# Cross-attention block on one core: the shift of b1 by four transfers ahead of the first feed-forward, first-layer chunks moved around transposes, and a last step with context and low scores together

## The chip, the core and the metric

The kernel runs on one core of a Trainium2 chip. A core has five instruction streams: TensorE (PE, with PEld for its weight loads), VectorE (DVE), ScalarE (ACT), GpSimd (POOL) and SyncE (SP, which here only issues transfers). SP and ACT each issue DMAs on a queue of their own. The metric is device microseconds of one execution; lower is better.

## The reference, cut to what matters

128 independent sequences of 128 tokens with 256 features, 16 heads of 16, a feed-forward of 1024, all in float32. The mask lets a query attend only to strictly earlier keys, and token 0 attends to nothing.

```python
q = (query @ Wq + bq); k = (key @ Wk + bk); v = (values @ Wv + bv)      # split in 16 heads
scores = jnp.einsum('bhqd,bhkd->bhqk', q, k) / jnp.sqrt(jnp.float32(D_K))
allowed = j < i + mask                                                  # mask == 0
attn = jax.nn.softmax(jnp.where(allowed, scores, NEG_INF), axis=-1)
attn = attn.at[:, :, 0, :].set(0.0)
ctx = jnp.einsum('bhqk,bhkd->bhqd', attn, v)
x = layer_norm(query + ctx @ Wo + bo, ln1_g, ln1_b)
ffn = jax.nn.relu(x @ W1 + b1) @ W2 + b2
out = layer_norm(x + ffn, ln2_g, ln2_b)
```

## The kernel before

Two sequences form a pair p; there are 64 pairs (NP = 64). The order of instructions on every engine is written out by hand: the calls in the source are the order of each engine's stream, and nothing reorders them. Each stream is worked off in order, so an instruction that waits holds back all that stands behind it on its engine, DMA issues included.

Work is pipelined over pairs. `step(p)` (line 785, p = 2 to 62) computes the scores and the softmax of pair p, the context, output projection and first norm of pair p-1, the first feed-forward layer of pair p-2 and the second layer and last norm of pair p-3; it also projects queries, keys and values of pair p+1. Lines 671 to 776 are the start-up (pairs 0 and 1), lines 885 to 971 the last step (pair 63) and what drains the pipeline behind it. The pieces named below are:

- `scores(p, hi)`, L326: `hi` = 1 is the upper half of the queries (128 keys), `hi` = 0 the lower half (64 keys). Then `mask` (DVE, L345), `maximum` (DVE L356, POOL L357), `exponential` (ACT, L364), `sums` (DVE L376 and L377, POOL L378).
- The probabilities are transposed. In the loop DVE does it in blocks of 32 (`turn`, L391, tile `tb`) and `bring` (L406) moves the blocks into `pT` by 16 DMAs, eight issued by SP and eight by ACT. For pairs 0, 1 and 63 `turn_on_pe` transposes on PE (L421) and ACT copies the result into `pT` (L423).
- `weigh` (L438, L448) multiplies `pT` with the values into `pc`; its first matmuls already read the lower half's part of `pT`. `context` (L460) copies `pc` to `cxT` on ACT, `attention_out` (L467) projects it, `attention_sum` and `attention_stats` (DVE, POOL) and `norm1` (DVE, L507) follow.
- `turn_x1` transposes the normed tile on DVE and by DMAs (x1t L237, x1T L240); `turn_x1_on_pe` (L226 on PE, copies on ACT L623 for pair 0, L628 else) is used for pairs 0 and 63.
- `hidden(p, fs)` (L638) is the first layer, two 128-wide chunks of the 1024 to one PSUM bank (eight matmuls as the trace counts them), with bias and relu on ACT (L644). `second` (L656) is the second layer; `second_sum`, `stats`, `scale_and_shift` (POOL: ve, sd, nb; L487, L488, L528), `norm2` (ACT, L536), `finish` (POOL, L542 and L543) and `store` (a DMA issued by ACT, L551) end a pair.

The first norm's gain and shift are folded into the first layer: W1 is scaled in place by `scale_w1` in step 3, and b1 gets be1 @ W1 added. `fold_norm1` computes be1 @ W1 by matmuls with one output row each (L566, 16 as the trace counts them), four side by side, and copies the four rows to `b1s` on ACT (L572). `add_b1` brings the 1024 numbers into a column layout `b1e_c` [128, 8] by eight DMAs on SP (L578). Pair 0 uses the unscaled W1 and the plain b1; the first reader of `b1e_c` is an addition on POOL in step 3 (L831). In step 2 both calls stand behind `scores(2, 0)`, and the first layer of pair 0 is cut in two: chunks 0 to 3 between the start-up's transposes, chunks 4 to 7 at the end of the step.

PSUM tiles of one bank come from a pool of four in turn (`bank`), those of two banks from a pool of two (`pair`). The built program gives every SP and ACT transfer one of eight completion semaphores in turn, in the order in which transfers stand in one list for both queues. A transfer waits at its issue until the one eight places before it in this list has landed, on whichever queue that was.

Of the kernel before, what the change touches and what calls it, by code (L numbers as in the profile page):

```python
# [10 lines left out]
ALU = mybir.AluOpType  # L11
AX = mybir.AxisListType

P = 128
NEG_INF = -1e30
LN_EPS = 1e-5
# [3 lines left out]
def tile_cross_attention_block(  # L20
# [22 lines left out]
    nc = tc.nc  # L43
# [308 lines left out]
    def maximum(p, hi, part):  # L352
        st = states[p]
        n = P if hi else HP
        sm, nmx = st["sm", hi], st["nmx", hi]
        nc.vector.tensor_reduce(nmx[:, part], sm[:, part, :], AX.X, ALU.max, negate=True)  # L356
        nc.gpsimd.tensor_tensor(  # L357
            sm[:, part, :], sm[:, part, :],
            nmx[:, part, None].to_broadcast([P, part.stop - part.start, n]), ALU.add,
        )  # L360

    def exponential(p, hi, part):
        sm = states[p]["sm", hi]
        nc.scalar.activation(sm[:, part, :], sm[:, part, :], AF.Exp)  # L364
# [132 lines left out]
    def attention_stats(p):  # L497
        stats(p, states[p]["t1"], 1)
        deviation(p, 1)
# [59 lines left out]
    def fold_norm1():  # L559


        ps = bank("ps_b1")
        n = DFF // NS
        for k in range(KC):
            for j in range(NS):
                nc.tensor.matmul(  # L566
                    ps[32 * j : 32 * j + 1, :n], be1_c[:, k : k + 1],
                    w1[:, k, j * n : (j + 1) * n], start=(k == 0), stop=(k == KC - 1),
                )
        for j in range(NS):  # L570
            at = slice(32 * j, 32 * j + 1)
            nc.scalar.copy(b1s[at], ps[at, :n])  # L572

    def add_b1():

        for f in range(FC):
            j, u = f // 2, f % 2
            nc.sync.dma_start(  # L578
                b1e_c[:, f : f + 1], b1s[32 * j : 32 * j + 1, u * P : (u + 1) * P]
            )  # L580

    def scale_w1():
# [30 lines left out]
    def turn_x1_on_pe(p):  # L613
        st = states[p]
        x1T = ffn.tile([P, NS, 4 * 32], F32, tag="x1T", name=f"x1T_{p}")
        st["x1T"] = x1T.rearrange("p i (s k a) -> p s i k a", s=2, k=KC)
        pt = transposed(st["x1"], f"ptn_{p}").rearrange(
            "p (k s i a) -> p k s i a", k=KC, s=2, i=NS
        )
        for k in range(KC):  # L620
            if p == 0:

                nc.scalar.activation(  # L623
                    st["x1T"][:, :, :, k, :], pt[:, k], AF.Identity,
                    bias=be1_c[:, k : k + 1], scale=g1_c[:, k : k + 1],
                )
            else:
                nc.scalar.copy(st["x1T"][:, :, :, k, :], pt[:, k])  # L628

    def hidden(p, fs, between=None):  # L630
        st = states[p]
        if fs[0] == 0:
            st["hT"] = ffn.tile([P, FC, TP], F32, tag="hT", name=f"hT_{p}")
        for f in fs[::2]:
            ph = bank(f"ph_{p}_{f}")
            for i in range(2):
                for k in range(KC):
                    nc.tensor.matmul(  # L638
                        ph[:, i * TP : (i + 1) * TP].rearrange("p (s i a) -> p s i a", s=2, a=32),
                        w1[:, k, (f + i) * P : (f + i + 1) * P], st["x1T"][:, :, :, k, :],  # L640
                        start=(k == 0), stop=(k == KC - 1),
                    )
            for i in range(2):
                nc.scalar.activation(  # L644
                    st["hT"][:, f + i, :], ph[:, i * TP : (i + 1) * TP], AF.Relu,
                    bias=(b1e_c if p else b1_c)[:, f + i : f + i + 1], scale=1.0,
                )
            if between:
                between(f)
# [135 lines left out]
    def step(p):  # L785
        nonlocal waiting
        if p > 2:
            load_ahead(p)
        scores(p, 1)
        mask(p, 1, 0)  # L790
        maximum(p, 1, ONE)
        if p > 2:
            second(p - 3, 0)
            mask(p, 1, 1)
            maximum(p, 1, TWO)
            exponential(p, 1, ONE)
            second(p - 3, 1)
            if p + 2 < NP:
                tokens(p + 2, "c")
        else:  # L800
            turn_x1_on_pe(0)
            hidden(0, range(FC // 2))
            turn_on_pe(1, 1, range(2))
            mask(p, 1, 1)
            maximum(p, 1, TWO)
            exponential(p, 1, ONE)
            turn_on_pe(1, 1, range(2, 4))
            turn_on_pe(1, 0, range(2))
            for which in "xc":
                tokens(3, which)  # L810
            add_bo(1)
            load_ahead(2)
            load_tokens(2)
        summed = []
        sums(p, 1, ONE)
        exponential(p, 1, TWO)
        if p > 2:
            second_sum(p - 3)
            summed = [p - 3]
        sums(p, 1, TWO)  # L820


        weigh(p - 1)
        context(p - 1)
        scores(p, 0)
        if p == 2:
            fold_norm1()
            add_b1()
        if p == 3:
            scale_w1()  # L830
            nc.gpsimd.tensor_tensor(b1e_c, b1e_c, b1_c, ALU.add)  # L831
        queries(p + 1)
        mask(p, 0, 0)
        mask(p, 0, 1)
        maximum(p, 0, ALL)
        exponential(p, 0, ALL)
        turn(p, 1, 0)
        turn(p, 1, 1)
        for q in waiting:
            finish(q)  # L840
        if p == 2:
            add_bo(2)
        attention_out(p - 1)
        attention_sum(p - 1)
        sums(p, 0, ALL)
        attention_stats(p - 1)
        if p + 2 < NP:
            tokens(p + 2, "x")
            if p == 2:
                tokens(p + 2, "c")  # L850
        turn(p, 0, 0)
        bring(p, nc.sync, range(NS * NS // 2))
        keys(p + 1)
        norm1(p - 1)
        turn_x1(p - 1)
        values(p + 1)
        values_out(p + 1)
        for q in waiting:
            store(q)
        add_bo(p + 1)  # L860
        if p == 2:
            residual1(0)
        residual1(p - 1)
        for q in summed:
            stats(q, states[q]["t2"], 2)
        for q in summed:
            scale_and_shift(q)
        at = NS * NS // 2

        def share(f):  # L870
            nonlocal at
            n = NS * NS - at if f == FC - 2 else 0 if f == 0 or p == 2 else NS // 2
            bring(p, nc.scalar, range(at, at + n))
            at += n

        hidden(p - 2, range(0 if p > 2 else FC // 2, FC), share)
        for q in summed:
            norm2(q)
        waiting = summed
# [5 lines left out]
    p = NP - 1  # L885
# [3 lines left out]
    second(p - 3, 0)  # L889
    mask(p, 1, 1)  # L890
    maximum(p, 1, TWO)
    scores(p, 0)
    mask(p, 0, 0)
    mask(p, 0, 1)
    exponential(p, 1, ONE)
    maximum(p, 0, ALL)
    exponential(p, 1, TWO)
    second(p - 3, 1)
    sums(p, 1, ONE)
    sums(p, 1, TWO)  # L900
    second_sum(p - 3)
    exponential(p, 0, ALL)
    sums(p, 0, ALL)
    finish(p - 4)
    weigh(p - 1)
    context(p - 1)
    attention_out(p - 1)
    attention_sum(p - 1)
    attention_stats(p - 1)
    norm1(p - 1)  # L910
    turn_x1(p - 1)
# [1 line left out]
    residual1(p - 1)  # L913
    stats(p - 3, states[p - 3]["t2"], 2)
    scale_and_shift(p - 3)
    hidden(p - 2, range(FC))
    turn_on_pe(p, 1, range(4))
    norm2(p - 3)

# [10 lines left out]
    attention_sum(p)  # L930
    attention_stats(p)
    second_sum(p - 2)
    hidden(p - 1, range(FC))
    norm1(p)
    stats(p - 2, states[p - 2]["t2"], 2)
    turn_x1_on_pe(p)
    residual1(p)
    scale_and_shift(p - 2)
    hidden(p, range(FC // 2))
# [15 lines left out]
    for s in range(2):  # L955
        py = bank(f"py_last_{s}")
        for f in range(FC):
            nc.tensor.matmul(
                py[:, :D], st["hT"][:, f, s * P : (s + 1) * P], w2[:, f, :],
                start=(f == 0), stop=(f == FC - 1),  # L960
            )
        nc.vector.tensor_tensor(t2[:, s], py[:, :D], st["x1b"][:, s], ALU.add)
        bs = small.tile([P, 6], F32, tag="bs", name=f"bs_last_{s}", bufs=4)
        mv = small.tile([P, 2], F32, tag="mvl", name=f"mv_last_{s}")
        nc.vector.bn_stats(bs, t2[:, s])
        nc.vector.bn_aggr(mv, bs)
        sd = small.tile([P, 1], F32, tag="sdl", name=f"sd_last_{s}")
        nc.gpsimd.tensor_scalar(sd, mv[:, 1:2], LN_EPS, None, ALU.add)
        nc.gpsimd.tensor_tensor(sd, sd, power[:, 0], ALU.pow)
        norm_alone(t2[:, s], mv[:, 0:1], sd)  # L970
        nc.sync.dma_start(out[2 * NP - 2 + s], t2[:, s])
# [35 lines left out]
```

## Time and profile before

| what | value |
|---|---|
| median of three runs | 1601.18 us (1600.74 to 1602.05) |
| profiled execution | 1598.13 us |
| its span, first to last instruction | 1596.4 us |
| PE busy | 1574.0 us, 99% of the span |
| DVE busy | 1372.2 us, 86% |
| POOL busy | 1282.6 us, 80% |
| ACT busy | 755.9 us, 47% |
| mean granted TensorE clock | 0.998 |
| distance of two steps in the loop (first-layer starts at 1471.58 and 1495.85) | 24.27 us |
| from the first matmul of `pc` to the first layer, in the loop (1510.84 to 1519.95) | 9.11 us |
| the same in step 3 (76.55 to 87.20) | 10.65 us |

A row of the timeline has the start and the duration in microseconds, the engine, the source line, the operation, output and inputs with their sizes, how many instructions are merged in it, and in brackets the idle time before it with what ended it. PE, PEld, DVE, ACT and POOL are the engines' work; SPq and ACTq are the issuing of DMAs. A wait is put down to the releaser that came last by the profile.

### The profile page before, as it was taken

The page shows a single profiled execution, that of the slowest core. Times are in us where ns is not written, and L with a number is a line of the kernel's source. Part 1 is how long each engine was busy: PE and PEld are TensorE (multiplying, and loading weights), DVE is VectorE, ACT ScalarE, POOL GpSimd, SP SyncE. Part 2 cuts the span into 40 slices and gives each one's busy share as a digit, 9 for nine tenths or more (in the row PEclk, how much of TensorE's full clock was granted, in tenths as well). Part 3 has the DMA queues.
Part 4 walks back from the last instruction along what each step waited for, and adds up shares of the span by engine and source line. Part 5 has one row for each costly group of instructions (what it writes and reads, how often), then busy time and mean ns, then how long its engine had stood idle before and what let it go on. Part 6 is the DMA issues. An engine that isn't in the chain of part 4 may idle for free.

```text
span 1596.4 us, 41271 instructions
## 1 busy us (share of the span) xinstructions
PE 1574.0 (99%) x16512; PEld 1327.7 (83%) x16512; DVE 1372.2 (86%) x1988; ACT 755.9 (47%) x1498; POOL 1282.6 (80%) x1106
## 2 busy tenths in 40 slices
PE   8899999999999999999999999999999999999998
PEld 6688888888888888888888888888888888888887
DVE  7889898888888998898988988888888889889862
ACT  5554454454444444444545444544444455454442
POOL 6878888888887888888888888878878888888882
PEclk9999999999999999999999999999999999999999
DMA  9356656556556556565565565565555655654430
GB/s 195 84 134 136 150 128 137 138 117 155 133 130 146 126 137 156 130 137 135 128 146 146 120 143 141 120 156 131 132 140 123 146 146 133 144 132 109 115 85 26
DMA packets 480511, 210.12 MB, mean 132 GB/s; under 512 B 349248, under 2 KB 448832, under 8 KB 480320
## 3 DMA queue, kind: packets, MB, share of 16 engines
q1 hardware_dynamic: 371952, 134.55, 37.9%
q10 hardware_dynamic: 108368, 72.92, 17.6%
q8 instruction: 131, 2.15, 0.6%
q14 instruction: 60, 0.49, 0.1%
HBM read 70.00 MB, written 33.03 MB: 65 GB/s over the span
## 4 chain that ended last, share of the span: by engine, by line
PE 95%; POOL 1%; DVE 1%; ACT 1%; DMA 1%; issue 0%; SPq 0%; POOLq 0%; ACTq 0%; DVEq 0%
PE ph L638 27%; PE py L656 27%; PE pq L260 8%; PE po L467 7%; PE pk L260 7%; PE pv L292 7%; PE pss L326 6%; PE pc L448 4%; PE pc L438 2%; POOL sm L357 0%; POOL sm L378 0%; ACT pT L423 0%; DMA pT<-tb 0%; DVE nmx L356 0%; DVE sm L345 0%
## 5 line engine op out<-in xcount | busy, mean ns | idle before, releaser
L357 POOL TENSOR_TENSOR sm<-sm,nmx 128x1024 f32<-128x1024 f32 x192 | 364.2, 1897 | 122.0 <-DVE nmx L356 121.1
L638 PE MATMUL ph<-x1T,w 128*128 128x256 f32 x2048 | 453.0, 379 | 2.4 <-ACT x1T L623 1.6
L656 PE MATMUL py<-w,hT 128*128 128x256 f32 x2016 | 452.8, 382 | 0.0
L378 POOL TENSOR_TENSOR sm<-sm,rs 128x1024 f32<-128x1024 f32 x192 | 364.3, 1899 | 93.6 <-DVE rs L377 89.6
L656 PEld LDWEIGHTS py<-w,hT 128*128 128x128 f32 x2016 | 377.6, 190 | 72.8 <-issue 16.7
L638 PEld LDWEIGHTS ph<-x1T,w 128*128 128x128 f32 x2048 | 388.9, 190 | 55.8 <-ACT x1T L623 2.0
L644 ACT ACTIVATE hT<-ph,b1e_c 128x256 f32<-128x256 f32 x504 | 208.2, 471 | 206.1 <-PE ph L638 104.8
L364 ACT ACTIVATE sm<-sm 128x1024 f32<-128x1024 f32 x192 | 200.8, 1054 | 206.5 <-POOL sm L357 206.1
L376 DVE TENSOR_REDUCE su<-sm 128x8 f32<-128x1024 f32 (+1 forms) x192 | 233.7, 1217 | 69.7 <-ACT sm L364 67.5
L345 DVE TENSOR_TENSOR sm<-pss,neg 128x1024 f32<-128x1024 f32 (+1 forms) x256 | 235.2, 940 | 52.2 <-PE pss L326 51.9
L391 DVE STREAM_TRANSPOSE tb<-sm 128x1024 f32<-128x1024 f32 x183 | 220.0, 1227 | 28.1 <-POOL sm L378 28.1
L356 DVE TENSOR_REDUCE nmx<-sm 128x8 f32<-128x1024 f32 (+1 forms) x192 | 234.3, 1220 | 6.6
L536 ACT ACTIVATE t<-t,nb,sd 128x256 f32<-128x256 f32 x124 | 67.7, 593 | 187.4 <-DMA pT<-tb 124.7
L260 PE MATMUL pq<-xT,wq 128*128 128x256 f32 x512 | 127.6, 392 | 0.0
L467 PE MATMUL po<-wo,cxT 128*128 128x256 f32 x512 | 121.2, 379 | 1.5 <-ACT cxT L460 1.4
L282 ACT ACTIVATE kT<-pk,bkh,half 128x256 f32<-128x256 f32 x252 | 120.6, 558 | 1.4 <-PE pk L260 1.4
L292 PE MATMUL pv<-wv,cT 128*128 128x256 f32 x512 | 121.0, 379 | 0.0
L260 PE MATMUL pk<-cT,wk 128*128 128x256 f32 x504 | 119.2, 379 | 0.0
L326 PE MATMUL pss<-kT,qT 32*64 32x256 f32 (+1 forms) x4096 | 116.8, 335 | 0.4 <-ACT kT L705 0.2
L271 ACT ACTIVATE qT<-pq,bqs_c 128x256 f32<-128x256 f32 x128 | 53.6, 470 | 122.8 <-PE pq L260 122.8
L260 PEld LDWEIGHTS pq<-xT,wq 128*128 128x128 f32 x512 | 92.4, 190 | 21.0 <-issue 10.9
L515 POOL TENSOR_TENSOR x1b<-x,g_r 128x512 f32<-128x512 f32 x64 | 81.7, 1277 | 34.9 <-DVE x L507 34.9
(92 smaller groups left out, 1765.9 us busy)
## 6 DMA issues: line engine op xcount, KB each, us to landing
pT<-tb ACTq DMA_DIRECT2D x488, 96.0 KB, 2.7
pT<-tb SPq DMA_DIRECT2D x488, 96.0 KB, 2.9
out_dram<-t ACTq DMA_DIRECT2D x63, 256.0 KB, 2.5
xb<-in_x_dram SPq DMA_DIRECT2D x124, 128.0 KB, 4.4
cb<-in_ctx_dram SPq DMA_DIRECT2D x124, 128.0 KB, 4.4
x<-in_x_dram SPq DMA_DIRECT2D x31, 512.0 KB, 4.9
x1t<-tbx SPq DMA_DIRECT2D x248, 64.0 KB, 2.3
x1T<-x1t SPq DMA_DIRECT2D x62, 256.0 KB, 3.2
```

What stands on the lines that cost most here:

```text
L260: nc.tensor.matmul(ps[:, m * TP : (m + 1) * TP], w[:, k, m * P : (m + 1) * P], src[:, k, :], start=(k == 0), stop=(k == KC - 1),)
L292: nc.tensor.matmul(pv[:, s * D : (s + 1) * D], st["cT"][:, k, s * P : (s + 1) * P], wv[:, k, :], start=(k == 0), stop=(k == KC - 1),)
L326: nc.tensor.matmul(sps[r // 2][s * HP : (s + 1) * HP, r % 2, m * 2 * n : (m + 1) * 2 * n].rearrange("p (e j) -> p e j", e=2), st["qT"][str ...
L345: nc.vector.tensor_tensor(st["sm", hi][:, part, :].rearrange("p (r n) j -> p r n j", r=2), st["sps", hi][t][:, :, : 4 * n].rearrange("p r ...
L356: nc.vector.tensor_reduce(nmx[:, part], sm[:, part, :], AX.X, ALU.max, negate=True)
L357: nc.gpsimd.tensor_tensor(sm[:, part, :], sm[:, part, :], nmx[:, part, None].to_broadcast([P, part.stop - part.start, n]), ALU.add,)
L376: nc.vector.tensor_reduce(su, sm[:, part, :], AX.X, ALU.add)
L378: nc.gpsimd.tensor_tensor(sm[:, part, :], sm[:, part, :], rs[:, :, None].to_broadcast([P, part.stop - part.start, n]), ALU.mult,)
L391: nc.vector.transpose(st["tb"][:, :, at : at + 256].rearrange("p j (n a) -> p n j a", a=32), st["sm", hi].rearrange("p h j -> p (h j)")[:, ...
L467: nc.tensor.matmul(po[:, s * D : (s + 1) * D], cxT[:, k, s, :], wo[:, k, :], start=(k == 0), stop=(k == KC - 1),)
L638: nc.tensor.matmul(ph[:, i * TP : (i + 1) * TP].rearrange("p (s i a) -> p s i a", s=2, a=32), w1[:, k, (f + i) * P : (f + i + 1) * P], st[ ...
L656: nc.tensor.matmul(st["py"][:, s * D : (s + 1) * D], st["hT"][:, f, s * P : (s + 1) * P], w2[:, f, :], start=(f == 0), stop=(f == FC - 1),)
```

## The change

Six edits, the first three in the start-up's step 2, the others at the end:

1. `fold_norm1` reads the moving operand in another order: columns u*128 + p of a quarter of W1 as (p, u), so that two consecutive elements lie 128 floats apart. The row in PSUM then has the two numbers of one partition side by side.
2. `add_b1` issues four DMAs in place of eight, each with two floats to a partition.
3. In step 2 both calls stand ahead of the first layer of pair 0 and behind the first two of pair 1's six transposes on PE; chunks 4 and 5 of that first layer move from the end of the step to a place before pair 1's last two transposes. On SP the four DMAs of b1 now stand ahead of the loads of the next inputs.
4. In the last step `second(60, 1)`, `weigh(62)` and `context(62)` stand ahead of `scores(63, 0)`, as in the loop; the first layer of pair 61 is cut, four chunks before `attention_out(62)` and four behind it; on POOL the lower half's subtraction and division stand later, the division behind `finish(59)`.
5. Behind it the transpose of pair 63's normed tile (`turn_x1_on_pe`) stands ahead of the last two chunks of pair 62's first layer.
6. In the last two norms the addition of epsilon goes from POOL to DVE.

```diff
@@ fold_norm1, add_b1
-                    ps[32 * j : 32 * j + 1, :n], be1_c[:, k : k + 1],
-                    w1[:, k, j * n : (j + 1) * n], start=(k == 0), stop=(k == KC - 1),
+                    ps[32 * j : 32 * j + 1, :n].rearrange("o (p u) -> o p u", p=P),
+                    be1_c[:, k : k + 1],
+                    w1[:, k, j * n : (j + 1) * n].rearrange("d (u p) -> d p u", p=P),
+                    start=(k == 0), stop=(k == KC - 1),
...
-        for f in range(FC):
-            j, u = f // 2, f % 2
+        for j in range(NS):
             nc.sync.dma_start(
-                b1e_c[:, f : f + 1], b1s[32 * j : 32 * j + 1, u * P : (u + 1) * P]
+                b1e_c[:, 2 * j : 2 * j + 2],
+                b1s[32 * j : 32 * j + 1].rearrange("o (p u) -> o p u", p=P),
             )
@@ step
             turn_x1_on_pe(0)
+            turn_on_pe(1, 1, range(2))
+            fold_norm1()
+            add_b1()
             hidden(0, range(FC // 2))
-            turn_on_pe(1, 1, range(2))
             mask(p, 1, 1)
             maximum(p, 1, TWO)
             exponential(p, 1, ONE)
             turn_on_pe(1, 1, range(2, 4))
+            hidden(0, range(FC // 2, 3 * FC // 4))
             turn_on_pe(1, 0, range(2))
...
-        if p == 2:
-            fold_norm1()
-            add_b1()
...
-        hidden(p - 2, range(0 if p > 2 else FC // 2, FC), share)
+        hidden(p - 2, range(0 if p > 2 else 3 * FC // 4, FC), share)
@@ the last step
     maximum(p, 1, TWO)
+    exponential(p, 1, ONE)
+    second(p - 3, 1)
+    sums(p, 1, ONE)
+    exponential(p, 1, TWO)
+    second_sum(p - 3)
+    sums(p, 1, TWO)
+    weigh(p - 1)
+    context(p - 1)
     scores(p, 0)
     mask(p, 0, 0)
     mask(p, 0, 1)
-    exponential(p, 1, ONE)
     maximum(p, 0, ALL)
-    exponential(p, 1, TWO)
-    second(p - 3, 1)
-    sums(p, 1, ONE)
-    sums(p, 1, TWO)
-    second_sum(p - 3)
+    hidden(p - 2, range(FC // 2))
     exponential(p, 0, ALL)
-    sums(p, 0, ALL)
     finish(p - 4)
-    weigh(p - 1)
-    context(p - 1)
     attention_out(p - 1)
     attention_sum(p - 1)
+    sums(p, 0, ALL)
     attention_stats(p - 1)
...
-    hidden(p - 2, range(FC))
+    hidden(p - 2, range(FC // 2, FC))
...
-    hidden(p - 1, range(FC))
+    hidden(p - 1, range(FC - 2))
     norm1(p)
     stats(p - 2, states[p - 2]["t2"], 2)
     turn_x1_on_pe(p)
+    hidden(p - 1, range(FC - 2, FC))
...
-        nc.gpsimd.tensor_scalar(sd, mv[:, 1:2], LN_EPS, None, ALU.add)
+        nc.vector.tensor_scalar(sd, mv[:, 1:2], LN_EPS, None, ALU.add)
```

In the last step p is 63. Behind the piece shown, both versions go on with `turn_on_pe(63, 1, range(4))`, `norm2(60)`, `turn_on_pe(63, 0, range(2))`, `finish(60)`, `store(60)`, `second(61, 0)`, `weigh(63)`. The order inside the loop for p = 3 to 62 is the same in both.

## The prediction

> **What bounds the kernel now.** I read the page's busy rows and chain first, then PE's waits, then the timeline where those waits fall, and last the granted clock there.
>
> ```profile
> PE 95%; POOL 1%; DVE 1%; ACT 1%; DMA 1%; issue 0%; SPq 0%; POOLq 0%; ACTq 0%; DVEq 0%
> ```
>
> The chain that ended last is PE. The loop repeats every 24.27 us with PE full, and no edit changes its order; only PE's waits in the start-up and the last steps can be won. All of PE's waits from the change's places:
>
> ```profile
> PE pc L438 <- DMA x1t<-tbx: 3.9, 1, 3.9
> ...
> PE pc L438 <- ACT pT L423: 2.3, 4, 1.7
> PE ph L638 <- ACT x1T L623: 1.6, 1, 1.6
> ...
> PE po L467 <- ACT cxT L460: 1.4, 1, 1.4
> PE ph L638 <- ACT x1T L628: 0.8, 1, 0.8
> ```
>
> Columns: total, times, longest. The largest, 3.9 us, is in step 3; its named releaser is a guess, since `pc` reads pT, not x1t. The timeline says what it is:
>
> ```profile
> 54.40 15.23 SPq L578 DMA_DIRECT2D b1e_c<-b1s  x8
> ...
> 69.73 5.12 SPq L406 DMA_DIRECT2D pT<-tb  x8
> ...
> 76.55 0.43 PE L438 MATMUL pc<-pT,vd 128*32 128x64 f32 x16 [3.89 <-DMA x1t<-tbx]
> ```
>
> The eight transfers of b1 hold SP until 69.63, though tb was complete at 63.87 (last transpose 62.67 + 1.20). SP's eight pT transfers follow; the last is issued at 69.73 + 5.12 - 0.6 = 74.25, and `pc` starts 2.3 us later. Most of the 15 us is one wait, for `vd` of pair 3:
>
> ```profile
> SPq L578 <- DMA vd<-vz: 8.9, 1, 8.9
> ```
>
> That is the rule of eight semaphores in turn. After the wait the clock is low (columns: window, length, PE busy, granted clock, DMA share, GB/s):
>
> ```profile
> 76.00:77.00 1.00, 0.45 (x33) 1.00 0.57 135
> 77.00:78.00 1.00, 1.00 (x57) 0.56 0.56 140
> 78.00:79.00 1.00, 1.00 (x41) 0.50 0.01 1
> 79.00:80.00 1.00, 1.00 (x33) 0.50 0.03 3
> 80.00:81.00 1.00, 1.00 (x4) 0.73 0.00 0
> ```
>
> From `pc` to the first layer step 3 takes 10.65 us, the loop 9.11: 1.54 us more.
>
> **Edits 1 to 3, before `pc` of step 3.** Before, PE waits 1.64 us at 42.29 for x1T. Now the 8 transposes (0.93 us) and the fold (0.97 us from 52.90 to the next start) stand there. The fold's bank is free at 41.77 (copies of pv), so it runs 41.85 to 42.8, beside x1T (until 42.69). Chunks 0 to 5 and the other transposes fill PE until 49.9. But ACT now does four b1s copies (1.53 us) and chunks 4 and 5 (0.84 us) ahead of pT's last copies: x1T to 42.69, two pT copies 43.8, b1s 45.3, hT 47.4, exponential 48.5, two copies 49.5, hT 50.3, two copies 51.35 against 50.76. So `pc(1)` ends 0.6 us later, but the fold (0.97) behind it is gone: queries(3) start at 53.45 against 53.87, and with chunks 4, 5 gone (1.73 us) scores(3) start at 62.3 against 64.43 and the second layer ends at 70.45 against 72.63. PE is 2.15 us ahead; its work was never the limit there.
>
> What is late next is the transfer of pT(2). exponential(2, 1, TWO) follows pT's copies on ACT, so sums, low mask and tb on DVE end at 64.5 (63.87 + 0.65). SP is then free: the b1 transfers are issued from 44 to 46.5, after each b1s copy; the loads behind them wait for DVE's transposes at 47.96 anyway, and the x load (one wait more, for the first xb load) goes out by 53. Cover gone, these cost nothing until 64.
>
> By the built program's order the list of transfers now reads vd(3), A1, a load, A2, A3, the x load, A4, A5, S1, A6, S2, A7, S3, A8, S4 to S8 (A and S: pT transfers of ACT and SP). Each waits for the eighth before it: S1 for vd(3), S3 for A3, S4 for A4, S5 for A5, S7 for A6. The old trace gives 2.4 us from issue to release (A1 at 64.60, A4, which waited for it, at 66.99) and 0.65 us per issue. A1 goes at 64.55, A3 at 66.0; S1 at 64.75 (vd 62.0 + 2.7), S2 65.4, S3 not before 66.0 + 2.4 = 68.4, then one per 0.65: S8 at 71.6. `pc(2)` starts at 71.6 + 2.27 = 73.9 instead of 76.55: **-2.65 us**, where a free SP queue would have given 5. PE idles 70.45 to 73.9, 3.45 us.
>
> Two prices are not in the trace. **The strided read of W1:** the nearest row is the fold with contiguous reads,
>
> ```profile
> 52.90 1.04 PE L566 MATMUL ps_b<-w,be_c 128*1 128x256 f32 x16
> ```
>
> that is 0.97 us. The Trainium skill, "SBUF — State Buffer", section "Door 1: The DMA port swizzle (why `[64,N]` ≈ `[32,N]`)", speaks against the edit: two successive accesses must fall into the same 16-byte line for full bandwidth, and here none do. By the row the sum is 0, by the rule, estimated as twice the time, +0.97, all of it on the path since ACT's b1s copies and the first layer follow. A gain is excluded, as no matmul is removed. I take 0, the only measured row; range 0 to +1.
>
> **The clock:** low from 76.9 to 80.3 after 3.89 us of idling, not low after 1.64 and 1.68. The Trainium skill, "TensorE: Matmul & The Clock Gate", section "Part 1: The HAM clock gate (the "warmup" mystery)", states half clock after an idle window of about 3.4 us, with windows running free. By the rule taken strictly 3.45 us would almost never hold a whole window, and 1.54 more would go; by the trace the window before the drop (3.4 us up to 76.9) held 0.4 us of work, so a not quite idle window is enough and 3.45 can trip it as 3.89 did. I take the row: 0, with -1.54 as the other end.
>
> **Edit 4, last step.** It begins as before at 1526.95, and up to the low scores it now stands as the loop's: `pc(62)` 1535.1, low scores 1536.6, chunks 0 to 3 of pair 61 at 1537.2 (its x1T, issued 1533.07, has 3.3 us of landing), po at 1540.67 without the 1.43 us wait for cxT, transposes at 1545.95 instead of 1547.79: 1.84 us early. They and the first half of the second layer end at 1552.2. (From here on the leading 15 is left out.) Then `pc(63)` needs ACT's last two pT copies, and these stand behind `norm2(60)`:
>
> ```profile
> 1551.28 0.50 POOL L528 TENSOR_SCALAR nb<-mv,sd 128x1 f32<-128x1 f32 x2
> ...
> 1551.58 1.09 ACT L536 ACTIVATE t<-t,nb,sd 128x256 f32<-128x256 f32 x2 [0.57 <-POOL nb L528]
> 1552.58 1.04 ACT L423 COPY pT<-ptp 128x512 f32<-128x512 f32 x2
> ...
> 1554.22 0.43 PE L438 MATMUL pc<-pT,vd 128*32 128x64 f32 x16
> ```
>
> nb ends POOL's row, and POOL starts it later: the low half's chain is now max 38.76 to 39.98, subtraction to 41.96, exponential to 43.04, then DVE's t1 sum (po ends 42.56) to 43.25, sum and reciprocal to 44.7, while POOL does `finish(59)` to 44.56; division 44.86 to 46.76, ve, sd to 47.83, DVE's norm 48.6, x1b to 51.35, ve(60) at 51.31 against 50.15: 1.16 us late. (All durations are the same lines' rows of before.) `norm2(60)` at 52.74, copies done 54.78 against 53.62. The rest of `pc(63)` follows, and the next matmul starts at 54.83 + 1.47 (the same stretch at 50.81 to 52.28) = 56.30 against 55.70. The stall of 1.43 goes, one of 2.1 comes: **+0.6 us**. If POOL were early enough the step would give -1.84; if 2.1 us of idling lowered the clock, +2.1.
>
> **Edits 5 and 6.** From the first layer of pair 62 to that of pair 63 it is 8.27 us (1560.98 to 1569.25); now 32 matmuls (6.91) and four transposes (0.5), the copies of x1T (0.65) lying beside the last chunk: 7.4, **-0.87**. Epsilon on POOL takes from 1591.88 to the power at 1592.48, with a hop of 0.28 before; on DVE the nearest row is a 128x2 tensor_scalar at 0.16 us: about -0.4 for each of two norms. The second norm's add (1590.70) follows directly on the first's last operation while PE has ended at 1590.23, so both count: **-0.8**, between -0.3 (DVE waits for PE) and -0.9.
>
> **Sum:** -2.65 + 0.6 - 0.87 - 0.8 = -3.7 us against the profiled 1598.13 (span 1596.4 and 1.73 around it): 1594.4. The median shown is 3.05 above the profiled run; the same difference on it gives **1597.5 us**.
>
> **Rivals.** *The clock holds:* 3.45 us of idling stays under the gate, or SP is a little quicker: -3.7 - 1.54 = -5.2, 1596.0. For it the strict rule, against it the window above. *The last step pays:* POOL's chain is 1.2 us shorter than I count, `pc(63)` waits for nothing: 2.4 more, 1595.1; against it the idle of 0.57 that ACT already has for nb. *Much of the gain is eaten:* the fold takes twice, or transfers land in 2.9 (the page's SP median) rather than 2.4 us, delaying S8 by 0.5, or the 2.1 us stall lowers the clock: -2, 1599.2. *Slower:* each of 60 loop steps pays for the changed list of transfers. Decides from 0.06 us a step (60 x 0.062 = 3.7); at 0.12 the time is 1601.18 + 3.5 = 1604.7. For it: vd's 8.9 us shows what one semaphore can hold. Against it: a transfer waits for the eighth before it whatever the number of its semaphore, and the loop's list is unchanged; pc's wait for pT is 0.4 us over the whole run, and the last pT lands (1504.88 + 2.37 + 2.7) 0.9 us before `pc` needs it.
>
> **How the numbers follow.** Forecast 0.40, its own range 1596 to 1599; clock holds 0.23; last step pays 0.08; gain eaten 0.20; slower 0.09. A change under 0.2% (3.2 us) cannot be told from none here. The forecast at -3.7 lies just beyond, I give it 0.65 of its chance: faster 0.26 + 0.23 + 0.08 and a little of the rest, 0.58; slower 0.10; same 0.32. Range: 1594.2 (clock holds, and the fastest ends of its terms) to 1601.2.
>
> **What would show it.** b1's four issues before 47; S3 about 2.4 us after A3 and SP's last pT issue at 71 to 72; one PE wait of 3 to 4 us at `pc` near 70.5 and half clock after it; L566 at about 1 us; `pc(63)` waiting some 2 us for ACT's pT; no wait at L628; steps of 24.27 us. Wrong if the PE wait in step 3 is under 2 us or over 4, or if the step length moved.

## The result, and the profile after

The changed kernel takes 1597.14 us (median of 12 runs, 1594.73 to 1599.43); the kernel before, in 12 runs that include the three shown above, takes 1599.99 us (1596.85 to 1603.77). The ratio is 0.9981, with a 95% interval of 0.9972 to 0.9990: 2.85 us less, 0.18%. The profiled execution of the changed kernel took 1598.49 us (span 1596.8, mean granted clock 0.996), 0.36 us more than that of the kernel before (1598.13, clock 0.998). It was one of the longer ones, and it shows why.

PE's waits (total, times, longest) now hold two large ones (the third line is from the start-up and as before), and the waits for x1T and cxT are gone:

```profile
PE pc L438 <- DMA pT<-tb: 3.8, 1, 3.8
PE pc L438 <- ACT pT L423: 3.6, 6, 2.2
PE ptp L421 <- POOL sm L378: 2.5, 3, 0.9
```

The first stands in step 3. The changed kernel's timeline there (here and below, rows of other instructions between those shown are left out):

```profile
42.12 1.26 PE L566 MATMUL ps_b<-w,be_c 128*1 128x256 f32 x16 [0.30 <-ACT vd L307]
43.31 3.72 PE L640 MATMUL ph<-x1T,w 128*128 128x256 f32 x16
43.82 1.52 ACT L574 COPY b1s<-ps_b 1x256 f32<-1x256 f32 x4
44.20 2.51 SPq L579 DMA_DIRECT2D b1e_c<-b1s  x4
...
64.67 5.13 ACTq L406 DMA_DIRECT2D pT<-tb  x8
64.85 7.79 SPq L406 DMA_DIRECT2D pT<-tb  x8
...
74.54 0.65 PE L438 MATMUL pc<-pT,vd 128*32 128x64 f32 x16 [3.83 <-DMA pT<-tb]
```

The four b1 issues are over at 46.7, and SP starts with pT 4.9 us earlier than before (64.85 against 69.73). But its eight issues take 7.79 us instead of 5.12. SP's own waits in this stretch say what held them, one wait for another pT transfer:

```profile
SPq L406 <- DMA pT<-tb: 2.6, 1, 2.6
```

So `pc` comes at 74.54 instead of 76.55. The start of a run differs by up to a few microseconds from execution to execution (the first transposes of `ptn`, just ahead of the change, stand at 39.99 before and 40.29 after), so I measure from ACT's first pT issue: 11.95 us to `pc` before (64.60 to 76.55), 9.87 after. That is 2.08 us won. Counted from the first transposes of `ptn`, where nothing has been changed yet, it is 2.31 (36.56 before, 34.25 after), since ACT's first issue itself comes 0.23 us sooner. Then the clock (window, length, PE busy, granted clock, DMA share, GB/s):

```profile
73.00:74.00 1.00, 0.00 (x0) 0.74 0.61 147
74.00:75.00 1.00, 0.46 (x20) 0.50 0.57 136
...
79.00:80.00 1.00, 1.00 (x4) 0.50 1.07 169
80.00:81.00 1.00, 1.00 (x5) 0.85 1.10 160
```

A window of 1 us at 0.74 had half clock for 0.52 us. So the clock falls already while PE idles, at about 73.5, and rises at about 80.3: 6.8 us at half, where the kernel before had 3.4 (77.12 to 80.53). From `pc` to the first layer, 9.11 us in the loop and 10.65 before, it takes 11.77, and the first layer starts at 86.31 instead of 87.20.

The second wait stands in the last step, the changed kernel's timeline:

```profile
1552.43 0.50 POOL L528 TENSOR_SCALAR nb<-mv,sd 128x1 f32<-128x1 f32 x2
...
1552.72 1.09 ACT L536 ACTIVATE t<-t,nb,sd 128x256 f32<-128x256 f32 x2 [3.88 <-POOL nb L528]
1553.72 1.04 ACT L423 COPY pT<-ptp 128x512 f32<-128x512 f32 x2
...
1554.34 0.31 PE L438 MATMUL pc<-pT,vd 128*32 128x64 f32 x4 [2.21 <-ACT pT L423]
...
1557.52 2.35 PE L658 MATMUL py<-w,hT 128*128 128x256 f32 x8
```

ACT idles 3.88 us in front of `norm2(60)`, which needs POOL's nb, while the transposes for its last two copies have long been ready; PE waits 2.21 us for these. And the clock falls once more, to which the 2.35 us of the last row and the 3.18 us from 1554.34 to it belong:

```profile
1554.00:1555.00 1.00, 0.49 (x12) 0.93 0.74 219
1555.00:1556.00 1.00, 1.00 (x46) 0.50 0.01 2
...
1558.00:1559.00 1.00, 1.00 (x5) 0.86 0.25 88
```

From the high scores of pair 63 to the end of the span (the tail, below) it takes 69.92 us, against 69.45 before. In this execution the tail edits lost 0.5 us.

### The profile page after: what moved, and what is told of

It reads as the page before. It is cut to its first block, busy times and chain, and to the rows that moved or that the text cites. A ratio compares the mean times of both kernels' runs of the same rounds, so it can differ in the third digit from the quotient of the medians.

```text
span 1596.8 us, 41276 instructions
## 1 busy us (share of the span) xinstructions
PE 1577.1 (99%) x16512; PEld 1332.5 (83%) x16512; DVE 1372.7 (86%) x1990; ACT 756.3 (47%) x1498; POOL 1282.1 (80%) x1104
```

## The experiments

Eleven kernels, each with runs of the kernel before beside it (kernels timed together share these); `fold_plain` alone has a single run, for its profile. A single profile is good for lengths between two instructions. From `ptn` to `pc` they repeat to 0.1 us where the code and the clock are the same, while from ACT's first pT issue to `pc` the two profiles with the old start differ by 0.3 (11.95 and 12.29). The medians carry intervals of about 0.1%, or 1.6 us.

### The start alone, and the tail alone

`start_only` is the changed kernel with the last steps of the kernel before; `end_only` is the kernel before with the last steps of the changed one.

> Edits 1 to 3 alone; the last steps are those of the kernel before. Theory (each edit brings its own part): pc of step 3 starts at 74.3 to 74.6 us instead of 76.55, with the third pT transfer of SP about 2.6 us after the second; the first layer of pair 1 starts at 86.0 to 86.5 instead of 87.20, because the half clock after the stall is paid in full; from the high scores of pair 63 to the end of the span 69.4 to 69.6 us, as before. Median about 1 to 2 us below before. Rival (the start brings nothing, the gain is in the tail): pc at 74.5 but the first layer of pair 1 at 87.0 or later, median within 0.5 us of before. Rival (the start brings everything): median 2.9 us below before.

> Edits 4 to 6 alone; the start is that of the kernel before. Theory: pc of step 3 at 76.5 us and the first layer of pair 1 at 87.2 as before; in the last step the last pc waits about 2.2 us for ACT's pT copies, as in the changed kernel, and the distance from the high scores of pair 63 to the end of the span is 68.2 us where the clock stays up and 69.9 where it falls after that wait, against 69.45 before. Median 0.5 to 1.5 us below before. Rival (the start brings everything): median not below before by more than 0.3 us. Rival (the tail brings everything): median 2.9 us below.

| kernel | median, us | ratio to before, 95% | ACT's first pT issue to pc, us | pc to first layer, us | tail, us |
|---|---|---|---|---|---|
| before | 1599.99 | | 11.95 | 10.65 | 69.45 |
| changed | 1597.14 | 0.9981, 0.9972 to 0.9990 | 9.87 | 11.77 | 69.92 |
| start_only | 1597.05 | 0.9984, 0.9974 to 0.9993 | 9.90 | 11.77 | 69.22 |
| end_only | 1599.74 | 1.0002, 0.9993 to 1.0011 | 12.29 | 10.68 | 69.88 |

The runs of the kernel before beside `start_only` and `end_only` have a median of 1599.43 us, and the ratios are to these. The start brings what the change brings; the tail edits together bring nothing that these runs can tell from zero, but the interval reaches from 1.1 us won to 1.8 us lost. For the start my theory expected 1 to 2 us, and it is 2.4; for the tail it expected 0.5 to 1.5, and the median misses that, as the first layer's time missed its forecast (85.68 in `start_only`, whose start was 0.7 us earlier than that of the changed kernel). The last `pc` waits 2.22 us in `end_only` too, and the clock falls there too.

`end_only` shows one thing more about the old start. In step 2 PE waits 1.64 us for x1T and 1.68 us for pT, as in the kernel before, but here the clock fell behind them, from 50.29 to 53.70. From `ptn` to the first layer of pair 1 it takes 49.11 us, against 47.21 before and 46.02 in the changed kernel, in which these two waits are gone.

### Which of the start's edits: the place or the number

`b1_late`: the four transfers at the old place.

```diff
             turn_on_pe(1, 1, range(2))
-            fold_norm1()
-            add_b1()
...
         scores(p, 0)
+        if p == 2:
+            fold_norm1()
+            add_b1()
```

> The changed kernel with the fold of b1 and its four transfers put back behind the low scores of pair 2: the number of transfers alone is changed in the start. Theory (what is left is the rotation of eight semaphores among SP's and ACT's transfers): by the list in the built program the fourth b1 transfer waits for ACT's first pT transfer, so it goes out at about 67 us, 2.4 us after that one (64.6); SP's pT transfers follow from 67.6, the third waits for ACT's fourth (to about 69), and the last is issued at about 72.3, as in the changed kernel (72.1): pc of step 3 at 74.6, against 74.54 in the changed kernel and 76.55 before. Rival (the place is what won the time, SP being free of b1 before tb is ready): SP's pT transfers start about 3 us later than in the changed kernel and all follow later, the last at 75, pc at 76.5 or later.

`b1_eight`: the new place, with the eight transfers and the contiguous read of the kernel before.

```diff
-        for j in range(NS):
+        for f in range(FC):
+            j, u = f // 2, f % 2
             nc.sync.dma_start(
-                b1e_c[:, 2 * j : 2 * j + 2],
-                b1s[32 * j : 32 * j + 1].rearrange("o (p u) -> o p u", p=P),
+                b1e_c[:, f : f + 1], b1s[32 * j : 32 * j + 1, u * P : (u + 1) * P]
             )
```

> The changed kernel with b1 in eight transfers of one column each and the contiguous read of W1, at the new place: the place alone is changed in the start. Theory (rotation): the eight transfers shift the list, the x load waits for vd of pair 3 until about 62 to 64 us, SP's first pT transfer waits for ACT's first until about 67, the third for ACT's fourth until about 69, and the last is issued at about 72.3: pc of step 3 at 74.6. Rival (the number is what won the time): pc at 76 or later. With b1_late at 74.6 as well, either edit alone would bring what both bring.

The timeline of `b1_late`:

```profile
65.68 5.34 ACTq L406 DMA_DIRECT2D pT<-tb  x8
...
67.90 0.47 SPq L579 DMA_DIRECT2D b1e_c<-b1s  x1
68.47 5.67 SPq L406 DMA_DIRECT2D pT<-tb  x8
...
76.03 0.66 PE L438 MATMUL pc<-pT,vd 128*32 128x64 f32 x16 [3.11 <-DMA pT<-tb]
```

and what its SP waited for, 50 to 77 us:

```profile
SPq L579 <- DMA pT<-tb: 9.6, 1, 9.6
```

The fourth b1 transfer does wait for ACT's first pT transfer, as the rotation of the eight semaphores says, and goes out 2.2 us after it. This execution had a later start (`ptn` at 41.75), so by distance: `pc` comes 10.35 us after ACT's first issue, which looks like 1.6 of the 2.1 us won. But ACT's first issue is itself 0.45 us closer to `ptn` here than in the changed kernel, where the fold and its copies stand ahead of it. From `ptn` to `pc` it is 34.28 us, so that the whole 2.3 us are won at the old place, as the theory said. The median is 1595.84 us, the ratio 0.9973 (0.9962 to 0.9985), not to be told from the changed kernel.

The timeline of `b1_eight`:

```profile
64.21 7.06 ACTq L406 DMA_DIRECT2D pT<-tb  x8
64.35 0.39 SPq L100 DMA_DIRECT2D x<-in_x_dram  x1
69.33 5.42 SPq L406 DMA_DIRECT2D pT<-tb  x8
...
76.44 0.65 PE L438 MATMUL pc<-pT,vd 128*32 128x64 f32 x16 [6.20 <-DMA pT<-tb]
```

its SP's wait ahead of the x load, and its DMA issues from 60 to 80 us (KB each, median us from issue to landing):

```profile
SPq L100 <- DMA vd<-vz: 11.9, 1, 11.9
```

```profile
pT<-tb ACTq DMA_DIRECT2D x8, 96.0 KB, 4.4
...
x<-in_x_dram SPq DMA_DIRECT2D x1, 512.0 KB, 5.4
```

Here `pc` comes where the rival had it, and in a way that neither had described. Four more transfers in the list put the x load on the semaphore of `vd(3)`, where b1's third transfer had been: it goes out at 64.35 instead of 50.9. That I had expected. Not expected was its company: its 512 KB now move beside ACT's pT transfers, whose landing takes 4.4 us in the median (2.5 in the changed kernel), and SP's first, waiting for ACT's first, goes out at 69.33, not at 67. `pc` comes 12.23 us after ACT's first issue, no better than the 11.95 before (from `ptn` 36.41 against 36.56), and the median says the same: 1599.43 us against 1600.41, ratio 0.9997 (0.9988 to 1.0007). So the new place without the smaller number brings nothing, and the smaller number at the old place brings all that is won at `pc`: what counts is which transfer stands eight places behind which. Both kernels keep the moved chunks and transposes of edit 3; a kernel with the smaller number alone was not run.

### The strided read

> The changed kernel with a contiguous read of W1 and contiguous write of PSUM in the fold; the order p, u is made in ACT's copies of b1s instead. Theory (the strided read costs a little, and nothing on the path): 16 matmuls of about 378 ns instead of 434, 0.97 us from the fold to the next matmul instead of 1.19, and pc of step 3 at the same distance behind ACT's first pT transfer (9.9 us) as in the changed kernel. Rival (the strided read delays the first layer and with it the transfers): pc 0.2 us or more closer.

```diff
-                    ps[32 * j : 32 * j + 1, :n].rearrange("o (p u) -> o p u", p=P),
-                    be1_c[:, k : k + 1],
-                    w1[:, k, j * n : (j + 1) * n].rearrange("d (u p) -> d p u", p=P),
+                    ps[32 * j : 32 * j + 1, :n], be1_c[:, k : k + 1],
+                    w1[:, k, j * n : (j + 1) * n],
...
-            nc.scalar.copy(b1s[at], ps[at, :n])
+            nc.scalar.copy(
+                b1s[at].rearrange("o (p u) -> o p u", p=P),
+                ps[at, :n].rearrange("o (u p) -> o p u", p=P),
+            )
```

It came as the theory had it, in one run. The fold of `fold_plain`, to be held against that of the changed kernel (1.26 us, next matmul 1.19 us after its start):

```profile
43.25 1.04 PE L566 MATMUL ps_b<-w,be_c 128*1 128x256 f32 x16 [0.31 <-ACT vd L307]
44.23 1.99 PE L642 MATMUL ph<-x1T,w 128*128 128x256 f32 x8
```

0.98 us to the next matmul: the stride costs 0.2 us, and `pc` comes 9.88 us after ACT's first issue, as with it.

### The wait of SP's third transfer

`split_6` changes only which queue carries how many of the sixteen pT transfers of step 2.

```diff
-        bring(p, nc.sync, range(NS * NS // 2))
+        bring(p, nc.sync, range(6 if p == 2 else NS * NS // 2))
...
-        at = NS * NS // 2
+        at = 6 if p == 2 else NS * NS // 2
```

> The changed kernel with, in step 2 alone, six of the sixteen pT transfers on SP and ten on ACT instead of eight and eight. Theory (SP's third transfer waits for ACT's third, then one goes out per 0.65 us): SP's sixth is issued at about 70.75 and ACT's tenth at about 71, so pc of step 3 starts at 73.2 to 73.5 instead of 74.54 and PE idles 2.6 us instead of 3.83; the clock may then fall later or not at all. Rival (the transfers' landing, not their issue, is the limit: bandwidth): pc at 74.3 or later.

The wait of SP for a pT transfer stays (2.8 us, once), fewer issues follow it, and `pc` comes 9.03 us after ACT's first issue instead of 9.87: 0.84 us won, where 1.1 to 1.3 was expected. So the order of issue sets `pc`, and landing has some share: from the last issue to `pc` it is 2.9 us here and 2.5 in the changed kernel. PE idles 2.84 us, and the clock falls all the same (10.78 us to the first layer). The median is 1596.03 us, 0.9982 (0.9970 to 0.9993).

### Filling the idle time ahead of pc

`queries_first` leaves the transfers alone and gives PE other work to do ahead of `pc`, in step 3 alone:

```diff
+        if p == 3:
+            queries(p + 1)
         weigh(p - 1)
         context(p - 1)
         scores(p, 0)
...
-        queries(p + 1)
+        if p != 3:
+            queries(p + 1)
```

> The changed kernel with, in step 3 alone, the queries of pair 4 ahead of the weighing of pair 2 on PE (and on ACT). Theory (PE's idle 3.8 us ahead of pc of step 3 comes from pT's transfers, and lowers the clock after it): pc still starts at 74.5 us, PE idles 2.1 us ahead of it, the first layer of pair 1 starts 1.7 us earlier (84.6) where the clock still falls for as long, 3.5 to 4.3 us earlier (82 to 82.8) where it does not; the next pc (step 4) can then wait up to 1 us for pT of pair 3. Median 1.7 to 3 us below the changed kernel. Rival (the stall is passed on: the step after is bound by pT's next transfer): the pc of step 4 waits for as much as was won, and the high scores of pair 4 to pc there take 9.9 us or more; median within 0.5 us of the changed kernel.

`pc` comes at the same distance (9.88 us) with 1.89 us of idling ahead of it, and in the profiled execution, the shortest of five, the clock holds. The windows of `queries_first` around it:

```profile
72.00:73.00 1.00, 0.00 (x0) 1.00 0.57 140
73.00:74.00 1.00, 0.41 (x29) 1.00 0.57 139
74.00:75.00 1.00, 1.00 (x83) 1.00 0.46 114
```

The first layer starts 41.81 us after the transposes of `ptn` (39.32 to 81.13) instead of 46.02 (40.29 to 86.31): 4.2 us earlier, 1.73 of it the queries, nearly all the rest the clock. The next `pc` waits for nothing and comes 8.15 us after its step's start, as in the loop. The median is 1593.33 us, 0.9963 (0.9950 to 0.9975): 6.1 us below the runs of before beside it, where the changed kernel was 2.85 below its own. So some 3 us are won (2.9 by the two ratios, whose intervals overlap at their ends), the upper end of what the theory gave.

In the last step this kernel has the changed kernel's wait, but here the clock held after it. Its timeline:

```profile
1549.41 0.31 PE L438 MATMUL pc<-pT,vd 128*32 128x64 f32 x4 [2.20 <-ACT pT L423]
...
1551.36 1.99 PE L658 MATMUL py<-w,hT 128*128 128x256 f32 x8
```

1.95 us instead of 3.18, and a tail of 68.67 us instead of 69.92. So the same 2.2 us of idling cost either nothing more or 1.2 us more; the last section says on what that depends.

### The last step's wait

`norm2_behind` moves `norm2(60)` behind the last two copies of pT:

```diff
     turn_on_pe(p, 1, range(4))
-    norm2(p - 3)
 
     p = NP - 1
     turn_on_pe(p, 0, range(2))
+    norm2(p - 3)
```

> The changed kernel with norm2 of pair 60 issued on ACT behind the last two copies of pT of pair 63 instead of ahead of them. Theory (the wait of pc is ACT's queue held by norm2, which waits for POOL's nb): the last pc starts at about 1552.2 us instead of 1554.34 without a wait over 0.3 us, the clock does not fall at 1555, and the distance from the high scores of pair 63 to the end of the span is 69.9 - 2.2 - 1.7 = 66.0 us; median 2.2 to 3.9 us below the changed kernel (ratio to before about 0.9960). Rival (the copies themselves, or POOL's norm chain, are late, and norm2 is only in between): the last pc still waits 1 us or more, and the next layer, of pair 62, waits for x1T, so that the end moves by less than 1 us.

Half of the theory came, and half did not. The timeline of `norm2_behind`:

```profile
1552.62 0.43 PE L438 MATMUL pc<-pT,vd 128*32 128x64 f32 x16
...
1553.29 1.09 ACT L536 ACTIVATE t<-t,nb,sd 128x256 f32<-128x256 f32 x2 [2.92 <-POOL nb L528]
...
1557.53 0.58 ACT L460 COPY cxT<-pc 128x508 f32<-128x508 f32 x1 [3.14 <-POOL t L543]
1558.16 2.42 PE L467 MATMUL po<-wo,cxT 128*128 128x256 f32 x8 [2.07 <-ACT cxT L460]
```

The last `pc` waits for nothing, as expected. But the next thing in ACT's queue behind `norm2` is the store of pair 60, which waits for POOL's `finish`, and behind that stands the copy of cxT: the wait has gone from `pc` to `po`, 2.07 us long, with a fall of the clock behind it. Tail 69.56 us; median 1596.10, 0.9977 (0.9969 to 0.9986).

`best` therefore puts `norm2(60)`, `finish(60)` and `store(60)` behind `context(63)`, on top of `queries_first`:

```diff
     turn_on_pe(p, 0, range(2))
-    norm2(p - 3)
-    finish(p - 3)
-    store(p - 3)
     second(p - 2, 0)
     weigh(p)
     context(p)
+    norm2(p - 3)
+    finish(p - 3)
+    store(p - 3)
```

(the lines are those of `norm2_behind`, from which they move.)

> queries_first, and in the last step norm2 of pair 60 (with finish and store) behind the context copy of pair 63 instead of ahead of the last pT copies. Theory (ACT's in-order queue held by norm2, which waits for POOL's nb, was what pc and, in norm2_behind, po waited for): neither the last pc nor the following po waits for ACT by more than 0.3 us, the clock stays up there, and from the high scores of pair 63 to the end of the span it takes 66.0 to 66.4 us, against 68.67 in queries_first and 69.45 before. Median 2.5 to 3.2 us below queries_first, ratio to before about 0.9945. Rival (the wait moves on once more: POOL's finish of pair 60, now later, holds the deviation of pair 63, or pair 62's first layer waits for x1T): a wait of 1 us or more at ptn or ph of the last pairs, 67.5 us or more.

Its timeline has neither wait:

```profile
1548.90 0.43 PE L438 MATMUL pc<-pT,vd 128*32 128x64 f32 x16
...
1550.57 0.58 ACT L460 COPY cxT<-pc 128x508 f32<-128x508 f32 x1 [3.91 <-PE pc L448]
1551.05 1.09 ACT L536 ACTIVATE t<-t,nb,sd 128x256 f32<-128x256 f32 x2
...
1552.21 1.89 PE L467 MATMUL po<-wo,cxT 128*128 128x256 f32 x8
```

The tail is 66.15 us, inside the 66.0 to 66.4 expected, 3.3 less than before the change. The median is **1590.55 us**, ratio 0.9942 (0.9930 to 0.9955): 9.7 us below the kernel before, over three times what the change brought.

`best_split_6` adds `split_6` to it.

> best, with the six and ten pT transfers of split_6 in step 2. Theory (issue of the transfers sets pc of step 3, and what is won there is kept): pc of step 3 about 0.85 us closer to ACT's first pT transfer (9.0 instead of 9.9 us) with 1 us of idling ahead of it, and the median 0.8 us below best. Rival (the next step's pc takes the stall over, since pT of pair 3 is not earlier): pc of step 4 waits 0.5 us or more for pT, and the high scores of pair 63 start no earlier than in best by more than the start of the run differs.

It takes 1590.43 us, 0.9941 (0.9929 to 0.9954), and so brings nothing to be seen. At the start `pc` is 0.5 us closer (9.42 instead of 9.91), not 0.85, and `pc` of step 4 doesn't wait, so the rival's reason isn't it either. In its profile the loop, from the high scores of pair 4 to those of pair 63, took 1434.7 us against 1433.2 in `best`; such differences of up to 2 us between executions, from single longer steps, occur among all the profiles here and hide half a microsecond. What became of it stays open.

### Edit 4 by itself

`edit4_undone` is `queries_first` with the last step of the kernel before, edits 5 and 6 kept: the lines of the last step's first half are those marked minus in the change.

```diff
-    exponential(p, 1, ONE)
-    second(p - 3, 1)
...
-    weigh(p - 1)
-    context(p - 1)
     scores(p, 0)
...
+    weigh(p - 1)
+    context(p - 1)
     attention_out(p - 1)
```

> queries_first with the order of the last step of the kernel before (edit 4 undone, edits 5 and 6 kept). Theory (edit 4 costs): from the high scores of pair 63 to the end of the span 67.6 us (34.0 to the first layer of pair 62 and 33.6 after it), against 68.67 in queries_first without a fall of the clock and 69.9 in the changed kernel with one; a wait of 1.4 us at po for cxT, none at the last pc; median 1.0 to 1.7 us below queries_first. Rival (edit 4 is worth what it took away, and the loss of the tail is in edits 5 and 6): 69 us or more, median at or above queries_first.

The 1.43 us wait for cxT is back,

```profile
1535.30 1.99 PE L467 MATMUL po<-wo,cxT 128*128 128x256 f32 x8 [1.43 <-ACT cxT L460]
```

and the tail takes 67.70 us, the 67.6 expected, with 34.06 us of it up to the first layer of pair 62. The median is 1592.61 us, 0.9952 (0.9938 to 0.9965): 0.7 us below `queries_first`, 1.8 by the two ratios, with intervals that overlap; the theory gave 1.0 to 1.7. By the traces edit 4, as it was made, costs 1.0 us where the clock holds (68.67 - 67.70) and 2.2 where it falls (69.92 - 67.70); the medians lean the same way without settling it.

## Why the prediction was right, and where it wasn't

The time came out 0.4 us from the forecast, the gain 0.85 us smaller than the sum: -2.85 instead of -3.7. The 1601.18 us that the sum was put on was itself 1.2 us above the median of twelve runs, and so the two misses cancelled: that the time fits to 0.4 us is luck. At 0.18% (0.10 to 0.28) the gain falls just short of the 0.2% that the text drew as its line.

**Edits 1 to 3: the mechanism was right, two terms too small.** Every sign named is there: b1's issues before 47, one wait of SP's third pT transfer for another pT transfer, one PE wait of 3.83 us (3.45 said), half clock behind it. Predicted were 2.65 us, measured 2.31 from `ptn` and 2.08 from ACT's first issue. The first term is "the old trace gives 2.4 us from issue to release": SP's third went out at 68.80, 2.85 us after ACT's third (65.95), and the rest of the chain moved with it. The second is the 2.27 us from SP's last issue to `pc`, which took 2.49 (72.05 to 74.54). The text's own rival "transfers land in 2.9" had the first. The text took the three edits as one; `b1_late` and `b1_eight` show that it was the number of transfers, and that "SP is then free" mattered less than who waits for whom.

**The strided fold: right.** 0.2 us, off the path; neither the 0.97 by the rule nor a delay of `pc`.

**The clock after `pc`: "I take the row: 0" was too simple.** The drop came, but its length changes: about 1.6 us lost in the two profiles with the old start (before, `end_only`), and 2.66, 2.66, 2.57 and 1.25 us in four with the new start (changed, `start_only`, `norm2_behind`, `fold_plain`). In the profiled execution 1.1 us of the 2.08 went back this way. The row was also read a little early: half clock lasted from 77.12 to 80.53, and the 3.41 us before it held 0.57 us of work, not 0.4. That "a not quite idle window is enough" stands.

**Two waits whose clock the text put at nothing.** The text has the kernel before "not low after 1.64 and 1.68", and that is one execution; in `end_only`, with the same start, the clock fell behind these two waits of step 2, and ACT's first pT issue came 1.5 us later after `ptn` (26.14 against 24.61). Edit 3 takes both waits away. In the traces the change brings the first layer of pair 1 forward by 1.2 us against the kernel before and by 3.1 against `end_only`; the median of `start_only` is 2.4 us lower. That some timed runs of the kernel before paid for this fall would fit, but is not shown.

**Edit 4: the stall was foreseen to a tenth, its consequence was not chosen.** "A stall of 2.1" was 2.21 at the place named and for the reason named, and the loss up to the first layer of pair 62 is 0.67 us where the clock held (34.70 us in `b1_late` and `b1_eight`, 34.03 before): the +0.6 of the text. In three more kernels, `queries_first`, `split_6` and `best`, x1T of pair 61 landed 0.3 to 0.5 us late on top, which the text had excluded by "3.3 us of landing". But the other end, "+2.1 if 2.1 us of idling lowered the clock", is what the profiled execution shows: 36.28 - 34.03 = 2.25. Of seven profiles with this wait three show it (changed, `end_only`, `fold_plain`), four don't; which of the two comes is decided by the grid of the clock's changes (last section). The step that failed is that this was put at nothing in the sum: as an estimate from these profiles, three in seven times 1.6 us (36.28 - 34.70), it is worth 0.7. The text had it in its rival "Much of the gain is eaten", with the landing in 2.9.

**Edits 5 and 6: right in kind, and near in size.** It is -1.02 us (said -0.87) from the first layer to the second layer of pair 62, and -0.55 (said -0.8) from the last second layer to the last operation of the norm, where POOL's power took 0.72 us instead of 0.57. From the first layer of pair 62 to the end of the span it is 35.42 us before and 33.64 after; 0.2 us of that difference lies behind the last operation, where only the last store is left, which these edits don't touch.

**The slower rival: not so.** The loop's step is 24.27 us in both.

So the tail's -1.07 became about zero in the medians (0.3 us above, with an interval that just reaches the forecast), since edit 4 takes back what 5 and 6 bring, in part by the clock; the start's 2.65 became about 2.4. The reason for the last step's loss, ACT's queue held by `norm2`, is shown by `best`; that the clock makes a difference between executions is shown by the windows of the profiles, while for the timed runs it is argued from the fact that of the changed kernel's twelve runs the three with a mean clock of 0.996 have spans of 1596.6 to 1597.7 us, the five with 0.999 have 1593.0 to 1595.7, and the four between lie on both sides.

## What to carry to other kernels

Where transfers share a few completion semaphores in turn, taking a transfer out shifts which of the rest wait for which, on both queues: read the list, not only the queue that you shorten. When a wait is moved off an engine, look at every instruction behind the one that still waits in the same in-order queue, stores included, or the wait turns up one place later. An idle PE can cost more than its length, by a fall of the clock that comes in some executions and not in others, so that one profile doesn't settle it; here, filling the idle time with work that was due anyway (`queries_first`, some 3 us) brought more than making the transfers faster (`split_6`, 0.84 us by its trace and nothing to be seen in the median).

## What the runs showed of the hardware

**The clock changes on a grid of 3.41 us.** In the records of the granted clock in all thirteen traces, the changes lie whole multiples of 3.41 us apart; in the changed kernel they stand at 73.48, 80.31, 1554.87 and 1558.28. Where the grid lies differs from one execution to the next. These are stretches of it, each with the one that follows, first in the changed kernel at the last `pc`:

```profile
1551.45:1554.87 3.42, 1.04 (x12) 1.00 0.36 98
1554.87:1558.28 3.41, 3.41 (x94) 0.50 0.24 83
```

then in `queries_first`, with the same wait of 2.2 us:

```profile
1548.36:1551.77 3.41, 2.18 (x98) 1.00 0.28 82
1551.77:1555.18 3.41, 3.41 (x18) 1.00 0.23 77
```

and in step 2 of `end_only`:

```profile
46.88:50.29 3.41, 1.55 (x37) 1.00 0.51 81
50.29:53.70 3.41, 3.41 (x119) 0.50 0.99 211
```

Behind the length of a stretch stands the time that PE was busy in it, and behind the bracket the granted clock. Of the some 6000 stretches at full clock, half clock followed all 13 in which PE was busy for less than 43% of the time, two of the four with 43 to 50%, and none above that. At half clock, another such stretch followed the four with PE busy for 14 to 69%, and full clock the fifteen with 78% or more. So whether a wait lowers the clock depends on how it falls on the grid: in the seven profiles with the same wait ahead of the last `pc`, PE was busy for 30 to 40% of the emptiest stretch in the three where the clock fell, and for 43 to 64% in the four where it held. The nine waits of 2.84 to 6.20 us ahead of `pc` of step 3 were all followed by a fall. Shorter waits were followed by one in some executions, down to those of 1.64 and 1.68 us in step 2 of `end_only`, and in the start-up of `best_split_6` two of 0.94 and 0.76 us in one stretch. A fall lasted 6.8 instead of 3.4 us where PE still idled for about a third or more of its first stretch (changed, `start_only`, `norm2_behind`, `b1_eight`). The Trainium skill, "TensorE: Matmul & The Clock Gate", Part 1, describes free-running windows of about 3.4 us and half clock after an idle one. The grid fits that; but the stretch need not be idle, as PE was busy for up to half of it.

**Transfers beside a large one.** In `b1_eight`, where a 512 KB load fell beside ACT's eight pT transfers of 96 KB, these landed in 4.4 us in the median, against 2.5 in the changed kernel; SP's eight, issued from 69.33 on, about when the load had landed (64.35 + 5.4), took 2.2. That the load is the cause is argued from this one profile.
